# Half of the attention weights turned by VectorE blocks and a DMA round trip in every attention, with the transfers pinned to one order

## The chip, the cores and the metric

The kernel runs on one core of a Trainium2 chip. The metric is device time in microseconds for one execution; a lower number is better. The matrix engine is PE (TensorE), the others DVE (VectorE), ACT (ScalarE), POOL (GpSimd) and SP (SyncE, whose queue issues all the transfers here). Data are fp32 throughout.

## The reference, cut to what matters

A tensor x of 8 batches x 256 tokens x 512 features goes through four layers, conditioned on a vector per batch:

```python
# layer 0: rotary attention, 8 query heads of 64, one key/value head; then a gated MLP
h = ada_rms(x, time_emb, ln1_w, ln1_tw)
q, k, v = apply_rope(heads(h @ Wq.T)), apply_rope(heads(h @ Wk.T)), heads(h @ Wv.T)
x = x + (softmax(q @ k.T / sqrt(64)) @ v) @ Wo.T
x = x + (silu(h2 @ Wg.T) * (h2 @ Wu.T)) @ Wd.T
# layer 1: attention with 16 heads of 32 and a bias, gated by gamma; then an MLP with gelu
p = softmax(qn @ kn.T + attn_bias); x = x + ((p @ v) @ Wproj.T + bproj) * gamma1
# layer 2: 16 query heads of 32 in 4 groups of keys; a sparse mask (window, every 64th key, no later block of 128)
scores = where(mask, -inf, q @ k_exp.T / sqrt(32)); x = x + (softmax(scores) @ v_exp) @ Wo.T
# layer 3: eight experts on 64 features each, a conditioned layer norm, an output product
```

What matters here is the softmax in the three attentions: its weights come out with queries on the partitions and keys along the row, and the product with v needs them with keys on the partitions, so every 128 x 128 block of weights has to be turned.

## The kernel before, in words

x stays on chip as 16 tiles of 128 tokens x 512. A batch is two of them (TB = 2, S = 256, KC = 4 chunks of features). The layers run one after the other; each attention is one call of `attend` (L667 on), each MLP one call of `mlp`, whose products are Strassen-like (L1002, L1051) and keep PE full.

**One attention.** `attend` loops over B x n_groups steps; a group is four heads (two groups a batch in attention0, four in attention1 and attention2). Step i does, in program order: the scores of its group (`scored`, L692, four heads at once on row tiles of PE); the first half of the PE transposes of the group before (`turned`, L769 and a copy back by DVE or ACT, L478 or L481); the softmax of its group; a share of the other work (`some`); the second half of the transposes; another share; the weighted sum of the group before (`weighted`, L794) and its division (`divided`, L811); a third share. The other work is a queue of generators: the projection of the next batch (`project0/1/2`, products L628, transposes of queries and keys L1236, L1242, L1453), the output product of the batch before, loads. `some(us)` draws from it until its budget is used or until a generator yields None; `rest()` runs it to the end, whatever it yields, and is called when a batch begins.

**Softmax.** Per head and query tile: a maximum (DVE, L714, or with bias or mask by a fused DVE instruction, L730), then exponentials with a running sum (ACT, L734). In attention0 and attention1, except in the last batch, heads 0 and 1 of a group are written in an order of 32 x 32 blocks, with the keys of the scores permuted to match; DVE then turns all blocks at once (L739, one STREAM_TRANSPOSE of 128 x 1024), and two transfers complete the turn: four puts to a scratch tile in DRAM (`put`, L546, "flip<-p") and one fetch back (L743, "p<-flip"). Heads 2 and 3 are turned by PE. In attention2 all four heads are turned by PE: with its mask a head has three blocks of 128 x 128 (384 columns), not four. The reciprocal of the sums (L745) is turned by DVE (L749), put to DRAM (L752) and fetched broadcast (L757).

**Inputs of the projections.** The normalised input of a batch, turned to features on partitions, is hT. In attention1 and attention2 `prepare` makes it two batches ahead: statistics on DVE, a power on POOL, the scaled rows written in block order (L468), a DVE block transpose (L532), four puts (L546, "turn<-hT"), and `fetch` (L564, eight fetches "hT<-turn", or one where the next stage takes blocks). `modulate` scales and shifts it (L488 on DVE, L489 on ACT) at the end of a batch. One step of it is drawn per group.

**Rotary tables.** `angles` (L1164 to L1196) reduces positions times frequencies to within pi by a chain of DVE instructions (`less`, L1176) and takes sines on ACT. It runs for batch 0, for batch 1, and, from `conditions(0)`, for all other batches at once.

**Order.** A scheduler sets each engine's order before the run, from a simulation: an instruction traced later may be issued earlier when its inputs are ready sooner. `keep_in_program_order(i)` pins i behind the instruction traced just before it on the same engine, without a wait. Before, it pins the weighted sums of turned heads and the modulation, and no transfer. Buffers: four of "p" (128 x 1024 each), two of hT, three of "row", eight of "wbig", four PSUM banks each of A and C.

Of the kernel before, what the change touches and what calls it, by code (L numbers as in the profile page):

```python
# [42 lines left out]
    "n": 4, "hT": 2, "qT": 2, "kT": 2, "v": 2, "ctxT": 4, "p": 4, "qk": 4, "row": 3, "wbig": 8,  # L43
# [54 lines left out]
def constants():  # L98
# [15 lines left out]
        "mask2": np.ascontiguousarray(mask),  # L114
    }
# [63 lines left out]
class Program:  # L179
# [21 lines left out]

    def bank(self, tag):
        return self.t([P, 512], tag)
# [26 lines left out]
    def setup(self):  # L230
# [41 lines left out]
        self.flips = [self.tc.dram_tile([P, 8 * P], F32, name=f"flip{i}") for i in range(4)]  # L272
        self.n_flip = 0
        self.half_pi = c([P, 1], "half_pi")
# [156 lines left out]
    def normed(self, *args):  # L431
        steps = self.norms(*args)
        while True:
            try:
                next(steps)
            except StopIteration as e:
                return e.value

    def norms(self, xs, eps, rms=False, outs=None):

# [16 lines left out]
        nc.gpsimd.tensor_tensor(r, r, self.neg_half[:, 0:n], ALU.pow)  # L457
        rows = []
        for i, x in enumerate(xs):
            yield  # L460
# [4 lines left out]
            if rms:  # L465
                nc.vector.tensor_scalar(y, x, r[:, i : i + 1], None, ALU.mult)
            else:
                nc.vector.tensor_scalar(  # L468
                    y, x, mv[:, i, 0:1], r[:, i : i + 1], ALU.subtract, ALU.mult
                )  # L470
            rows.append(y)
        return rows

# [43 lines left out]
    def prepare(self, name, b, quick=False):  # L517

        eps, _, _, _, rms, blocks = self.stage(name)
        xs = [self.x[TB * b + t] for t in range(TB)]
        hT = self.t([P, KC * S], "hT")
        self.ready[name, b] = [hT, None, None, math.inf, False]
        if quick:
            self.ready[name, b][3] = 0
            self.ready[name, b][1] = self.normed(xs, eps, rms)
            return
        nc = self.nc
        y = hT.rearrange("p (c k t i) -> p c k t i", c=4, k=KC, t=TB)  # L530
        yield from self.norms(xs, eps, rms, [y[:, :, :, t, :] for t in range(TB)])
        nc.vector.transpose(hT, hT)  # L532
        kept = self.turns[self.n_turn % 3]
        self.n_turn += 1
        self.put(kept, hT)
        self.ready[name, b][2] = kept

    def in_blocks(self, name, b):

        return 2 if name != "attention2" and b < B - 1 else 0  # L540

    def put(self, kept, tile):

        to = kept.rearrange("(c i) (a x) -> a i c x", c=4, a=4)
        for a in range(4):
            self.nc.sync.dma_start(  # L546
                to[a], tile[32 * a : 32 * a + 32, :].rearrange("p (c x) -> p c x", c=4)
            )

    def fetch(self, calls):  # L550

        for (name, b), entry in self.ready.items():
            hT, _, kept, _, _ = entry
            if kept is None:
                continue
            entry[2:4] = None, self.calls + calls
            if self.stage(name)[5]:
                self.nc.sync.dma_start(hT, kept)
                continue
            parts = kept.rearrange("p (a k t j) -> p k t a j", a=4, k=KC, t=TB)  # L560
            to = hT.rearrange("p (k t a j) -> p k t a j", k=KC, t=TB, a=4)
            for k in range(KC):
                for t in range(TB):
                    self.nc.sync.dma_start(to[:, k, t], parts[:, k, t])  # L564
# [15 lines left out]
    def modulate(self):  # L580

        for (name, b), entry in self.ready.items():
            hT, rows, kept, at, done = entry
            if rows is None and not done and at < math.inf:
# [3 lines left out]
                entry[3:] = 0, True  # L588

    def h(self, name, b, quick=False):  # L590


        if (name, b) not in self.ready:
            for _ in self.prepare(name, b, quick):
                pass
            yield None
            self.fetch(1)
        hT, rows, _, at, done = self.ready[name, b]
# [53 lines left out]
    def attend(self, name, n_groups, hd, project, value, finish, work, key_tiles=(2, 2), biased=None,  # L652
# [25 lines left out]
        got, ctx = self.got, {}  # L678
# [19 lines left out]
        def softmax(s, b):  # L698
            n_blocks = self.in_blocks(name, b)
# [1163 lines left out]
```

## Time and profile before

| what | value |
|---|---|
| median of 3 runs | 2105.07 us (2104.76 to 2105.3) |
| the profiled execution | 2102.78 us |
| its span on the core, granted TensorE clock | 2100.7 us, 0.989 |
| attention0 with the start | 0 to about 306 us |
| MLP 0 | about 306 to 880 |
| attention1 | about 915 to 1270 |
| MLP 1 | about 1270 to 1655 |
| attention2 | about 1686 to 1941 |
| experts | about 1941 to 2101 |
| PE transposes of weights, L769 | 816, 122.3 us listed |
| DVE block transposes of weights, L739 | 42 |
| flips: puts, fetches | 168 and 42 |

The span runs from the first to the last instruction. Busy times of PE include overlapping matmuls once; the mean time of one matmul (282 ns at L769) is longer than the step from one to the next, since they are pipelined. The stage bounds are read from the chain of work that ended last. A "q" after an engine's name is its instruction queue: for SP, the issue of a transfer, not its landing.

### The profile page before, as it was taken

To read this page: it belongs to the slowest core of one execution; us is meant where nothing else is said; L and a number is where in the kernel's file an instruction comes from. 1 tells how busy PE (TensorE), PEld (TensorE's weight loads), DVE (VectorE), ACT (ScalarE), POOL (GpSimd) and SP (SyncE) were. 2 spreads that over 40 slices of the span, in tenths; PEclk is the share of its full clock that TensorE was granted. 3 is DMA by queue.
4 is the path that set the end of the run, shared out by engine and by line. 5 is a ranking of instruction groups with operands and counts; after the bars stand their busy time and mean duration, and the time that the engine had idled before them with its cause. 6 is when DMAs were issued, how large, how long until landed. Compare 5 with 4: busy or idle time off the path is not lost.

```text
span 2100.7 us, 36220 instructions
## 1 busy us (share of the span) xinstructions
PE 2034.6 (97%) x12946; PEld 1486.9 (71%) x12946; DVE 1348.9 (64%) x4432; ACT 743.7 (35%) x2330; POOL 302.7 (14%) x340
## 2 busy tenths in 40 slices
PE   7799999999999999999999999999999999999999
PEld 4455569999999999854544448999999755555444
DVE  6677766666676555756676675767666777676233
ACT  4233421111111111146566652222222265556543
POOL 1111200000000000054445621000000111010220
PEclk8999999999999999999999999999999999999999
DMA  9543451212130010335455542235211321210001
GB/s 317 161 139 94 115 202 39 72 42 64 62 108 26 16 32 16 97 95 140 130 145 142 150 132 87 86 92 155 63 46 36 89 44 38 58 38 21 9 36 40
DMA packets 202659, 182.48 MB, mean 87 GB/s; under 512 B 81200, under 2 KB 169200, under 8 KB 202480
## 3 DMA queue, kind: packets, MB, share of 16 engines
q1 hardware_dynamic: 202480, 180.17, 29.3%
q8 instruction: 103, 1.69, 0.3%
q14 instruction: 76, 0.62, 0.1%
HBM read 122.16 MB, written 57.97 MB: 86 GB/s over the span
## 4 chain that ended last, share of the span: by engine, by line
PE 82%; DVE 6%; ACT 6%; DMA 3%; POOL 2%; issue 1%; SPq 0%; ACTq 0%; DVEq 0%; POOLq 0%
PE C L1002 28%; PE C L628 21%; PE A L1051 18%; ACT p L734 4%; PE A L692 4%; PE C L794 3%; PE C L769 3%; PE A L1731 1%; PE C L1750 1%; ACT p L481 1%; DVE st L448 1%; DVE p L730 1%; DMA hT<-turn 1%; PE C L315 1%; DVE n L647 1%
## 5 line engine op out<-in xcount | busy, mean ns | idle before, releaser
L1002 PE MATMUL C<-hT,wbig 128*128 128x128 f32 x3072 | 416.4, 275 | 1.0 <-DVE p L1025 1.0
L1002 PEld LDWEIGHTS C<-hT,wbig 128*128 128x128 f32 x3072 | 388.7, 192 | 10.1 <-issue 3.5
L628 PE MATMUL C<-wqkv,hT 128*128 128x512 f32 (+1 forms) x768 | 314.7, 551 | 0.4 <-ACT v L1490 0.4
L734 ACT ACTIVATE p<-p,low 128x256 f32<-128x256 f32 (+1 forms) x512 | 240.0, 471 | 165.8 <-DVE low L730 154.5
L1051 PE MATMUL A<-wbig,p 128*128 128x256 f32 x1024 | 242.2, 379 | 0.0
L628 PEld LDWEIGHTS C<-wqkv,hT 128*128 128x128 f32 x768 | 131.7, 193 | 122.7 <-issue 108.7
L1051 PEld LDWEIGHTS A<-wbig,p 128*128 128x128 f32 x1024 | 189.7, 190 | 23.1
L1032 DVE TENSOR_TENSOR p<-p,C 128x256 f32<-128x256 f32 x192 | 79.0, 419 | 164.3 <-PE C L1002 162.3
L1022 ACT COPY p<-C 128x128 f32<-128x128 f32 x192 | 50.8, 265 | 367.5 <-PE C L1002 359.0
L628 PE MATMUL C<-wo,ctxT 128*128 128x512 f32 x336 | 159.8, 609 | 2.9 <-DVE ctxT L811 2.9
L1002 PE MATMUL C<-ctxT,wbig 128*128 128x128 f32 x1152 | 160.0, 275 | 0.0
L1002 PE MATMUL C<-qk,wbig 128*128 128x128 f32 x1152 | 159.8, 275 | 0.0
L456 POOL TENSOR_SCALAR r<-mv 128x2 f32<-128x2 f32 (+1 forms) x28 | 7.0, 252 | 967.7 <-DVE mv L449 967.7
L730 DVE CUSTOM_DVE_ANT_0 p<-A,row 128x256 f32<-128x256 f32 (+1 forms) x400 | 127.8, 377 | 26.6 <-PE A L692 24.9
L1002 PEld LDWEIGHTS C<-ctxT,wbig 128*128 128x128 f32 x1152 | 144.1, 192 | 0.0
L1002 PEld LDWEIGHTS C<-qk,wbig 128*128 128x128 f32 x1152 | 144.0, 192 | 0.0
L769 PEld LDWEIGHTS C<-ident,p 128*128 128x128 f32 x816 | 92.2, 142 | 64.3 <-issue 37.8
L769 PE MATMUL C<-ident,p 128*128 128x128 f32 x816 | 122.3, 282 | 4.8 <-DVE p L478 1.9
L1374 ACT ACTIVATE p<-C 128x128 f32<-128x128 f32 x64 | 17.7, 277 | 302.4 <-DVE p L1032 302.4
L1023 DVE TENSOR_TENSOR p<-p,C 128x128 f32<-128x128 f32 x192 | 54.7, 285 | 96.6 <-ACT p L1022 95.6
L628 PEld LDWEIGHTS C<-wo,ctxT 128*128 128x128 f32 x336 | 59.5, 191 | 67.7 <-issue 55.2
L734 ACT ACTIVATION_READ_ACCUMULATOR p<-p,low 128x1 f32 x512 | 96.2, 188 | 0.0
(227 smaller groups left out, 3224.6 us busy)
## 6 DMA issues: line engine op xcount, KB each, us to landing
flip<-p SPq DMA_DIRECT2D x168, 128.0 KB
p<-flip SPq DMA_DIRECT2D x42, 512.0 KB
turn<-hT SPq DMA_DIRECT2D x120, 128.0 KB
hT<-turn SPq DMA_DIRECT2D x16, 512.0 KB
kept<-hT SPq DMA_DIRECT2D x16, 512.0 KB
hT<-kept SPq DMA_DIRECT2D x16, 512.0 KB
wbig<-spread SPq DMA_DIRECT2D x64, 128.0 KB
hT<-turn SPq DMA_DIRECT2D x112, 64.0 KB
```

The source lines that it names most:

```text
L315: self.nc.tensor.matmul(m[32 * i : 32 * i + 32, :], cond[:, k, :], w[c // 512][:, k, c % 512 : c % 512 + width], start=(k == 0), stop=(k = ...
L628: self.nc.tensor.matmul(out, lhsT(k), rhs(k), start=(k == 0), stop=(k == n - 1))
L692: nc.tensor.matmul(s[j][:, at[q] : at[q] + wide[q]], lhsT(q), keys, start=True, stop=True,)
L730: nc.vector.tensor_tensor_reduce(out, src, by, -1.0, BIG, ALU.add, ALU.min, low[:, q : q + 1])
L734: nc.scalar.activation(out, src, AF.Exp, bias=low[:, q : q + 1], scale=sign, accum_out=tot[:, j, q : q + 1],)
L769: nc.tensor.transpose(m[:, n * P : (n + 1) * P], p[:, at[q] + k * P : at[q] + (k + 1) * P], self.ident,)
L794: mm = nc.tensor.matmul(o[i * hd : (i + 1) * hd, c * S + q0 * P : (c + 1) * S], value(got[b][1], g, j, k), weights(j, mine), start=(k == 0 ...
L1002: nc.tensor.matmul(m[:, c : c + P], w[:, k * P : (k + 1) * P], b[:, k], start=(first and k == 0), stop=(k == steps - 1), skip_group_check= ...
L1022: nc.scalar.copy(g[:, 0, :], m[:, 0:P])
L1023: nc.vector.tensor_tensor(g[:, 0, :], g[:, 0, :], m[:, P : 2 * P], ALU.add)
L1032: nc.vector.tensor_tensor(g[:, 1:3, :], g[:, 0, :].unsqueeze(1).to_broadcast([P, 2, P]), m[:, 2 * P : 4 * P].rearrange("p (i t) -> p i t", ...
L1051: nc.tensor.matmul(acc[at][:, half * S : (half + 1) * S], left, right, start=(p == 0 and half == 0), stop=(p == 3), skip_group_check=True,)
```

## The change

1. **Attention2 turns half of its weights by blocks too**: `in_blocks` now gives 2 in all attentions but in the last batch; a second copy of the mask in block order is a new constant (`mask2_blocks`) and is loaded once. The mask and the small rotary table now share one "row" tile. The DVE transpose there is 128 x 768, its put and fetch 384 KB each.
2. **Transfers are pinned** by `queued`: puts of weights and of hT, fetches of both, the put and the broadcast fetch of the reciprocals. In a softmax the order is: puts of the weights; the put of the reciprocals; one step of a preparation; the fetch of the weights; the broadcast fetches.
3. **`prepare` goes in five steps**: statistics; scaling and block transpose; puts; the first half of the fetches; the second half. The first two are drawn after a softmax, the others inside one. For batch b + 3 it begins at the last group of batch b; `fetch` is gone.
4. **"p" is one tile of eight parts** of 512 columns, given out in a ring (`part`); a softmax takes four parts, a step of an MLP two.
5. **`angles` has become a generator** (`angle_steps`) with three yields, and each `less` is pinned.

The core of the diff:

```diff
+    def part(self, n):
+        if self.n_part == 0:
+            self.parts = self.t([P, 8 * 512], "p")
+        at = self.n_part % 8
+        self.n_part += n
+        return self.parts[:, at * 512 : (at + n) * 512]
...
+    def queued(self, dma):
+        return self.tc.keep_in_program_order(dma)
...
-        return 2 if name != "attention2" and b < B - 1 else 0
+        return 2 if b < B - 1 else 0
...
     def prepare(self, name, b, quick=False):
...
+        by = self.norms_of(xs, eps, rms)
+        yield
+        hT = self.t([P, KC * S], "hT")
...
+        self.over(xs, by, rms, [y[:, :, :, t, :] for t in range(TB)])
         nc.vector.transpose(hT, hT)
+        yield
         kept = self.turns[self.n_turn % 3]
         self.n_turn += 1
         self.put(kept, hT)
+        yield
+        if blocks:
+            self.queued(nc.sync.dma_start(hT, kept))
+        else:
...
             for k in range(KC):
                 for t in range(TB):
+                    self.queued(nc.sync.dma_start(to[:, k, t], parts[:, k, t]))
+                if k == KC // 2 - 1:
+                    yield
+        entry[2] = self.calls + 1
...
                 if j == 3 and n_blocks:
                     nc.vector.transpose(blocks, blocks)
...
                     self.put(kept, blocks)
-                    nc.sync.dma_start(blocks, kept)
+                    between.append((blocks, kept))
...
-            nc.sync.dma_start(kept.rearrange("c (b r) -> b c r", b=4), inv_t)
+            self.queued(nc.sync.dma_start(kept.rearrange("c (b r) -> b c r", b=4), inv_t))
+            for steps in preps:
+                if len(steps) <= 3:
+                    next(steps.pop(), None)
+            preps[:] = [steps for steps in preps if steps]
+            for to in between:
+                self.queued(nc.sync.dma_start(*to))
...
+                for steps in preps:
+                    if len(steps) > 3:
+                        next(steps.pop())
+                if ahead_of and g == 0 and b == 0:
+                    for _ in self.prepare(name, 1, quick=True):
+                        pass
+                    preps.append([self.prepare(name, 2)] * 5)
+                    for _ in range(2):
+                        next(preps[-1].pop())
+                elif ahead_of and g == n_groups - 1 and b + 3 <= B:
+                    if b + 3 < B:
+                        preps.append([self.prepare(name, b + 3)] * 5)
+                        next(preps[-1].pop())
+                    elif after is not None:
+                        preps.append([self.prepare(after, 0)] * 4)
+                        next(preps[-1][-1])
+                elif not ahead_of and g == 0 and b == B - 1:
+                    preps.append([self.prepare(after, 0)] * 4)
+                    for _ in range(3):
+                        next(preps[-1].pop())
...
         def less(out, k, c):
-            nc.vector.scalar_tensor_tensor(out, k, -c, ang, ALU.mult, ALU.add)
+            self.tc.keep_in_program_order(
+                nc.vector.scalar_tensor_tensor(out, k, -c, ang, ALU.mult, ALU.add)
+            )
...
-                self.angles(self.cos, self.sin, slice(2 * TB, NT))
+                yield from self.angle_steps(self.cos, self.sin, slice(2 * TB, NT))
...
+        both = self.bank("row")
...
+        self.mask = both[:, TB * 64 :]
         nc.sync.dma_start(self.mask, d["mask2"])
+        self.mask_blocks = self.bank("row")[:, :384]
+        nc.sync.dma_start(self.mask_blocks, d["mask2_blocks"])
...
-            biased=(self.mask,), extra={7: (self.expert_inputs(0), 1.74)},
+            biased=(self.mask, self.mask_blocks), extra={7: (self.expert_inputs(0), 1.74)},
```

## The prediction

> **What bounds the kernel now.** I read the page's first part, then the table by stage, then the timeline of one batch of attention2, then the chain of waits in its last group.
>
> ```profile
> PE 2034.6 (97%) x12946; PEld 1486.9 (71%) x12946; DVE 1348.9 (64%) x4432; ACT 743.7 (35%) x2330; POOL 302.7 (14%) x340
> ```
>
> PE is busy in 97% of the span, so time goes down only where PE loses work or idles. The stages, from the table of busy time by stretch (columns: stretch, length, then busy us and count of PE, PEld, DVE, ACT and POOL, the granted clock, DMA share, GB/s):
>
> ```profile
> 0.00:80.00 80.00, 54.00 (x311) 31.16 (x312) 51.91 (x176) 26.66 (x65) 12.53 (x32) 0.85 0.70 239
> 915.00:1270.00 355.00, 348.11 (x1910) 173.40 (x1911) 241.95 (x810) 207.25 (x665) 166.04 (x144) 0.99 0.49 135
> 1686.00:1941.00 255.00, 241.44 (x1719) 132.97 (x1716) 182.59 (x834) 147.18 (x586) 26.54 (x34) 1.00 0.17 40
> ```
>
> Attention1 (second row) already turns half of its weights by blocks and leaves PE idle for 7 us in 355, with the DMAs at 135 GB/s. Attention2 (third row) turns all by PE, idles 13.6 us in 255 and moves 40 GB/s. So PE bounds both, and attention2 has room on the DMAs. Its batches repeat every 34.44 us (the chain shows the same piece at 1746.87, 1781.31, 1815.75). In one of them, PE's timeline:
>
> ```profile
> 1753.46 0.94 PE L692 MATMUL A<-kT,qT 32*128 32x128 f32 x16
> 1754.33 0.88 PE L769 MATMUL C<-ident,p 128*128 128x128 f32 x6
> 1755.04 1.88 PE L628 MATMUL C<-wo,ctxT 128*128 128x512 f32 x4
> ...
> 1756.76 0.88 PE L769 MATMUL C<-ident,p 128*128 128x128 f32 x6
> 1757.56 0.48 PE L692 MATMUL A<-kT,qT 32*128 32x128 f32 x2
> ...
> 1759.89 0.86 PE L794 MATMUL C<-p,kT 128*32 128x256 f32 x16
> ```
>
> A group is scores (L692), six transposes (L769), products, six transposes, the weighted sum (L794). Six transposes last until the next start 0.71 us later, 118 ns each, though a single one is listed with 280 ns: they overlap.
>
> **What goes.** The page has 816 transposes at L769. Attention2 has 8 batches x 4 groups x 4 heads x 3 blocks = 384; in batches 0 to 6 two heads of four leave: 7 x 4 x 2 x 3 = 168. Over five batches (1712.65 to 1884.62) I summed the time from each L769 start to PE's next start: 30.89 us for 240, 128.7 ns each, small waits included. 168 x 128.7 ns = **21.6 us**. It is between 168 x 110 ns = 18.5 (the bare step between two) and 21.6.
>
> The Trainium skill speaks against the swap: "VectorE: DVE Perf Modes", Rules for kernel authors, says to transpose 128x128 on TensorE when PSUM will do; The three transpose paths gives 390 ns there against 311 ns on VectorE, for 32x32 blocks alone. At its 390 ns the sum would be 65 us saved; the trace's step is a third of that, and it decides.
>
> **What comes, beside other work.** VectorE per batch of attention2: the copies of two heads a group go (eight, 4.4 us), four STREAM_TRANSPOSE of 768 columns come. The trace has 1024 columns at 1.245 us and 32 at 0.204, so 768 is about 0.98: 3.9 us. Net -0.5 us on an engine with 24.7 busy of 34.4: nothing. ScalarE keeps eight copies of 384 columns a batch, since the two heads left both go to it: nothing. Scores and weighted sums read in block order: in attention1, where heads 0 and 1 do so already, four row-tiled matmuls of 256 columns take 196 to 220 ns with blocks or without: nothing. DMA: 28 groups x 2 x 393 KB = 22 MB in some 240 us, 92 GB/s on top of 40, less than attention1 carries: nothing in bandwidth. The ring for p has the room of the four buffers before (four of eight parts a softmax, as two of four tiles): nothing. Mask and rotary table share a tile; the count of row buffers is the same: nothing.
>
> **The rotary steps.** PE's longest stall is 10.31 us at 57.26, because ScalarE's sine (L1193) stands ahead of two copies and waits 16.3 us for VectorE:
>
> ```profile
> 47.69 1.28 ACT L1193 ACT_TABLE_LOAD   x1
> 65.27 0.52 ACT L1193 ACTIVATE row<-row 128x384 f32<-128x384 f32 x1 [16.30 <-DVE row L1192]
> ```
>
> Each pinned `less` is tied to VectorE's instruction traced just before. By the code `conditions(0)` is drawn first inside `rest()` at batch 1, which doesn't stop at a yield, so that is the chain's own predecessor, which it needs anyway. The pins order nothing new. Bounds: -10.3 (the stall goes) to +10.3 (another such order in the neighbouring softmax). I take 0, because the chain and what is around it are traced as before.
>
> **What is late next: the last group.** The four groups' scores start at 1745.02, 1753.46, 1762.59, 1769.73, the next batch's at 1779.46. The chain of waits in the last one:
>
> ```profile
> 1771.08 1.86 ACT p L734 x8
> ...
> 1773.30 1.77 ACT p L734 x8
> 1775.08 0.02 issue
> 1775.10 0.04 DVE inv L745
> ...
> 1776.01 0.34 DVE n L647
> 1776.36 0.07 issue
> 1776.42 1.28 POOL qk L1650
> 1777.70 0.04 issue
> 1777.75 0.67 PE C L1236 x4
> ```
>
> Here PE isn't the limit: exponentials, VectorE's rope behind the reciprocal, POOL's sum, and only then the transposes of the next queries. Taking six transposes out of this iteration brings nothing: 7 x 6 x 128.7 ns = **5.4 us** of the 21.6 don't arrive. (Bounds: 0, were the scheduler to put rope first; 7 x 0.98 = 6.9 more, were the block transpose to stand in this chain.)
>
> **The blocks' way.** A way in attention1, on SP's queue:
>
> ```profile
> 1099.54 1.75 SPq L546 DMA_DIRECT2D flip<-p  x4
> 1101.40 0.55 SPq L752 DMA_DIRECT2D spread<-invT  x1
> ...
> 1103.31 0.34 SPq L743 DMA_DIRECT2D p<-flip  x1
> ```
>
> The scores were at 1093.66; the transpose ran 1098.27 to 1099.52; the last put was issued 1100.85 to 1101.30 and the fetch at 1103.31; the chain elsewhere shows a fetch landing in 3.38 us. For attention2, with T the start of a group's scores: two heads' maxima by T+2.1 and exponentials by T+3.3, transpose until T+4.5 (ScalarE's row: about 0.88 us a head), puts issued until T+6.3. The pinned order now is: puts, spread (T+6.3 to 6.9, since exponentials end at T+5.2 and the reciprocal's transpose at T+6.1), one step of a preparation, then the fetch. That step is four puts of hT (0.45 us each) or four fetches (0.61 each, the row of L564: 628 ns), so the fetch is issued at T+8.5 without one, T+8.7 after puts, T+9.3 after fetches, and lands some 2.9 us later, T+11.4 to T+12.2. Scores to own weighted sum lasts now 14.9, 15.5, 11.7 and 14.9 us; with 0.7 us less an iteration 13.4, 14.0, 10.3 and 13.5. Only the third group is short, by 1.9 us. PE already idles there for 0.54 + 0.73 us a batch, so I charge 1.9 - 1.27 = 0.6 x 7 = **4.4 us** (bounds 0, if PE's static order puts products first, and 1.9 x 7 = 13).
>
> "DMA: Bandwidth & Descriptors" of the Trainium skill, Anatomy of one DMA, gives 2.0 us and bytes at 436 GB/s for one DMA, so 2 x 2.9 = 5.8 us there and back. By that estimate the third group would land at T+10.3, just in time, and the 4.4 us would fall away; the trace's two trips, 2.5 and 3.4 us after issues that queue, are what I count.
>
> **hT.** Its fetch used to float (in attention2 issued at 1757 to 1764.6, long before the next batch's products at 1781.15). Pinned, its second half goes behind the spread of the last group. In attention1: 1135.05 + 4 x 0.61 = 1137.5; packets of such a fetch end 1.7 us after the last issue; 0.4 us for the modulation (L488): 1139.6. The products start at 1138.43 and need that half after two steps of 0.45 us, at 1139.3. Short by 0.3 to 0.8 us, five batches: I charge 0.4 x 5 = **2 us** (bounds 0 and 4). In attention2 it is ready at T+9.3+1.7+0.4 = T+11.4 and needed at T+9.0 (next scores) + 0.94 + 0.4 (three transposes) + 0.43 = T+10.8; the 0.6 us it lacks is covered by the delay charged above, uncovered it costs 0.6 x 5 = 3. Behind such a wait PE's queue holds the weighted sum, pinned after those products; on VectorE and ScalarE the modulation, pinned too, holds up the next softmax where it stands before it.
>
> Attention0 keeps its transposes and blocks; pinning puts its flips behind loads that preceded them before too (flip at 150.47, after the weights' loads): 0, bounds -3 and +10.
>
> **Sum.** -21.6 + 5.4 + 4.4 + 2 = -9.8 on the profiled execution's 2102.78 us (span 2100.7): 2093.0. The median of the runs shown, 2105.07, is 2.29 higher: **2095 us**.
>
> **Rivals.** *All of it arrives:* the scheduler fills every wait: 2105 - 21.6 = 2083; without the sine's stall too, 2073. For it: attention1 shows no PE gap over 0.15 us in its middle batches. Against it: attention2 has 16.4 us of products a batch to fill with, attention1 28.5. *It cancels out,* the change waits taking the transposes' place: the last group's chain takes the block transpose (6.9), the third group's charge doubles (8.8): 2105 - 21.6 + 5.4 + 6.9 + 8.8 + 2 = 2106, no change. *Slower: SP's one queue in a fixed order.* The fetch of each group stands behind the preparation's issues, which themselves wait for transposes and landings; where such a wait is 2 us longer than reckoned, the three groups of a batch that have one hold PE up by 2 us each: 6 x 6 = 36 us in attention2 against 16 gained, 2125. It decides from about 2.3 us a batch on, 0.8 us for each of the three. For it: puts of hT took 3.1 us to land (issued until 1753.96, fetch at 1757.15) and in attention1 fetches already held a flip back by 3 us (1112.68 to 1115.87). Against it: those cost PE nothing.
>
> **Chances.** Forecast 0.42 (2089 to 2100), all of it 0.22 (2070 to 2089), cancels 0.12, slower 0.24 (2110 to 2130). Two tenths per cent, 4.2 us, is about what a measurement here can tell from no change. So faster 0.64, same 0.12, slower 0.24. The range leaves out the tip of the gain and the upper half of the slower case: 2075 to 2118; the likeliest case's own is 2089 to 2100.
>
> **What would show it.** L769 at 648 instead of 816; in attention2 a period of 32.5 to 33.5 us; waits of L794 for p<-flip in third groups; the next queries' L1236 still behind POOL; the 10 us stall at 57 still there; small waits of L628 for hT in attention1. Wrong if the period stays at 34.4 or falls under 31.5, if the early stall vanishes, or if PE waits for flips in attention0 or 1.

## The result and the profile after

The changed kernel takes 2118.89 us (median of 4 runs, 2117.78 to 2123.94) against 2105.19 us before (4 runs beside it): a ratio of 1.0063, 95% interval 1.0039 to 1.0087. It is slower, by some 13 us, where 2095 was forecast. The profiled execution is the longest of the four, 2123.94 us, with a span of 2122.1 and a granted TensorE clock of 0.981 (before 0.989); so the trace shows some 5 us more loss than the median has.

Three rows first, from the page's busy times, its list of groups and its DMA issues, of the changed kernel:

```profile
PE 2027.6 (96%) x12778; PEld 1479.0 (70%) x12778; DVE 1351.5 (64%) x4404; ACT 746.6 (35%) x2330; POOL 304.8 (14%) x340
...
L790 PE MATMUL C<-ident,p 128*128 128x128 f32 x648 | 102.7, 286 | 7.0 <-DVE ctxT L833 3.6
...
p<-flip SPq DMA_DIRECT2D x28, 384.0 KB
```

The work did leave: 168 transposes fewer (L790 is L769 of before), 28 fetches of 384 KB more, PE busy for 7 us less. Yet the span grew by 21. So PE idles. The table of busy time by stretch, for the same three stages (columns as in the prediction; the stretches are moved and lengthened with the stages):

```profile
0.00:80.00 80.00, 54.60 (x300) 32.05 (x302) 50.76 (x173) 26.12 (x63) 12.58 (x32) 0.85 0.71 244
916.00:1280.00 364.00, 352.31 (x1931) 174.58 (x1931) 240.26 (x811) 207.90 (x665) 167.17 (x145) 0.99 0.52 136
1695.00:1962.00 267.00, 231.25 (x1551) 123.61 (x1550) 185.62 (x808) 148.65 (x585) 28.64 (x36) 0.94 0.50 124
```

Attention2 (third row) leaves PE idle for 36 us of 267, where it was 13.6 of 255, and the granted clock fell there from 1.00 to 0.94. A lower clock beside a less busy PE is the second thing to see in this row. For all that follows I take each attention from its first to its last scores: attention1 went from 336.8 to 343.5 us, attention2 from 263.2 to 275.1. Another 4 us are in attention0, which differs by as much between executions with the same order of instructions (below).

What PE waited for in attention2, from the waits of before and of after (us in total, times, longest):

```profile
PE C L1236 <- POOL qk L1650: 4.4, 6, 0.8
PE C L794 <- ACT p L481: 4.1, 7, 0.8
PE A L692 <- DVE low L730: 3.6, 1, 3.6
```

```profile
PE C L816 <- ACT p L491: 11.0, 7, 2.5
PE C L816 <- DMA p<-flip: 5.5, 2, 2.8
PE A L709 <- DVE qT L489: 4.6, 5, 3.4
PE C L816 <- DVE st L449: 4.4, 1, 4.4
PE C L1276 <- DVE ctxT L833: 4.2, 3, 1.9
```

The weighted sum (L816, L794 of before) waited for 4.1 us; now for 20.9. One of these waits, in PE's timeline of after, in a last group (the weights are the third group's):

```profile
1789.74 0.60 PE L1690 MATMUL C<-wqkv,n 128*128 128x256 f32 x2
1792.77 1.28 PE L816 MATMUL C<-p,kT 128*32 128x256 f32 x16 [2.44 <-ACT p L491]
1793.98 1.11 PE L1270 MATMUL C<-ident,qk 128*128 128x128 f32 x4
1794.88 0.42 PE L1276 MATMUL C<-ident,kr 128*128 128x128 f32 x1
1795.10 1.06 PE L1270 MATMUL C<-ident,qk 128*128 128x128 f32 x4
1797.45 0.31 PE L1276 MATMUL C<-ident,kr 128*128 128x128 f32 x1 [1.29 <-DVE ctxT L833]
```

SP's queue shows why the sum had to wait:

```profile
1784.12 1.82 SPq L576 DMA_DIRECT2D flip<-p  x4
1786.05 0.55 SPq L766 DMA_DIRECT2D spread<-invT  x1
1786.64 2.56 SPq L558 DMA_DIRECT2D hT<-turn  x4
1789.36 0.50 SPq L772 DMA_DIRECT2D p<-flip  x1
```

The four fetches of hT take 2.56 us to issue, ahead of the fetch of the weights. That one lands 3.22 us after its issue (the chain of waits), at 1792.58; the copy of the two heads that PE turned, put behind the exponentials on ScalarE, ends at 1792.77. The view puts the wait down to the copy, but the fetch alone would have held the sum as long: third groups wait in batches 0 to 5, 17.3 us in all, and in all six the sum begins 0.13 to 0.14 us after the last record of the fetch's landing in the trace. Behind the wait the weighted sum lasts 1.28 us instead of 0.86 and four L1270 1.11 instead of 0.66: PE runs at half clock (the records of the clock have 0.50 from 1793.14 to 1796.55).

### The profile page after: what moved, and what is told of

It is laid out like the page before. It is cut to its first block, busy times and chain, and to the rows that moved or that the text cites. A ratio compares the mean times of both kernels' runs of the same rounds, so it can differ in the third digit from the quotient of the medians.

```text
span 2122.1 us, 36171 instructions
## 1 busy us (share of the span) xinstructions
PE 2027.6 (96%) x12778; PEld 1479.0 (70%) x12778; DVE 1351.5 (64%) x4404; ACT 746.6 (35%) x2330; POOL 304.8 (14%) x340
## 3 DMA queue, kind: packets, MB, share of 16 engines
q1 hardware_dynamic: 222784, 202.40, 33.3%
## 4 chain that ended last, share of the span: by engine, by line
PE 81%; DVE 7%; ACT 4%; DMA 4%; POOL 2%; issue 1%; SPq 1%; ACTq 0%; DVEq 0%; POOLq 0%
PE C L1028 28%; PE C L645 21%; PE A L1077 18%; PE A L709 4%; ACT p L748 3%; PE C L816 3%; PE C L790 2%; PE A L1769 1%; DVE p L744 1%; PE C L1788 1%; DMA hT<-turn 1%; DMA p<-flip 1%; DMA wbig<-spread 1%; DVE st L449 1%; DVE hT L474 1%
## 5 line engine op out<-in xcount | busy, mean ns | idle before, releaser
L645 PE MATMUL C<-wqkv,hT 128*128 128x512 f32 (+1 forms) x768 | 319.2, 554 | 4.7 <-DVE hT L498 2.7
L645 PEld LDWEIGHTS C<-wqkv,hT 128*128 128x128 f32 x768 | 131.9, 194 | 127.8 <-issue 105.7
L645 PE MATMUL C<-wo,ctxT 128*128 128x512 f32 x336 | 159.0, 608 | 3.2 <-DVE ctxT L833 2.6
L790 PEld LDWEIGHTS C<-ident,p 128*128 128x128 f32 x648 | 75.0, 143 | 62.3 <-issue 39.9
L790 PE MATMUL C<-ident,p 128*128 128x128 f32 x648 | 102.7, 286 | 7.0 <-DVE ctxT L833 3.6
L645 PEld LDWEIGHTS C<-wo,ctxT 128*128 128x128 f32 x336 | 59.7, 191 | 67.7 <-issue 52.9
L709 PE MATMUL A<-kT,qT 32*128 32x256 f32 (+2 forms) x896 | 90.6, 406 | 8.5 <-DVE low L744 4.9
```

The source lines that it names most:

```text
L645: self.nc.tensor.matmul(out, lhsT(k), rhs(k), start=(k == 0), stop=(k == n - 1))
L709: nc.tensor.matmul(s[j][:, at[q] : at[q] + wide[q]], lhsT(q), keys, start=True, stop=True,)
L790: nc.tensor.transpose(m[:, n * P : (n + 1) * P], p[:, at[q] + k * P : at[q] + (k + 1) * P], self.ident,)
```

## Theories and experiments

Two theories stood at the beginning. **O**: the pinned order of transfers costs the time (the slower rival). **R**: the round trip of the weights is too long for attention2 in any order. A third came after the first four runs. **F**: it is too long for the third group only, and the half clock behind its wait adds to the price. Whether **the rotary pins** matter is answered by unpinned, which keeps them.

All were timed beside the kernel before (medians 2104.64 to 2106.41), except gaps, which measures a cost by itself. Attention1 and attention2 are from first to last scores in one profile, idle is PE's in attention2, "busy at half" is PE's busy time there under half clock.

| kernel | median us | ratio (95%) | attention1 | attention2 | idle | busy at half |
|---|---|---|---|---|---|---|
| before | 2105.19 | | 336.8 | 263.2 | 16.3 | 6.0 |
| after | 2118.89 | 1.0063 (1.0039 to 1.0087) | 343.5 | 275.1 | 38.6 | 34.3 |
| blocks_alone | 2108.11 | 1.0012 (1.0003 to 1.0021) | 336.1 | 266.0 | 31.6 | 25.1 |
| no_blocks2 | 2108.65 | 1.0016 (1.0008 to 1.0025) | 342.4 | 266.7 | 16.8 | 11.4 |
| unpinned | 2105.38 | 0.9993 (0.9983 to 1.0002) | 335.2 | 263.4 | 33.3 | 23.5 |
| flip_first_early | 2117.4 | 1.0057 (1.0044 to 1.0070) | 343.7 | 270.5 | 31.0 | 35.9 |
| skip3_unpinned | 2097.07 | 0.9962 (0.9949 to 0.9974) | 335.7 | 258.0 | 21.0 | 19.8 |
| skip3_pinned | 2113.47 | 1.0041 (1.0028 to 1.0054) | 342.4 | 269.2 | 28.9 | 24.1 |
| free_hT | 2122.79 | 1.0084 (1.0071 to 1.0098) | 341.4 | 275.9 | 38.0 | 38.2 |
| pin_hT | 2114.46 | 1.0047 (1.0035 to 1.0060) | 345.7 | 269.0 | 34.0 | 35.6 |
| pin_flips | 2102.90 | 0.9991 (0.9982 to 1.0000) | 334.2 | 263.0 | 33.1 | 26.1 |
| skip3_old | 2096.99 | 0.9964 (0.9951 to 0.9976) | 336.7 | 258.5 | 24.8 | 16.8 |
| skip23_unpinned | 2094.85 | 0.9948 (0.9936 to 0.9961) | 335.3 | 254.8 | 17.6 | 10.6 |

Where attention2's time stands, from first scores of a batch to first scores of a later one, in us:

| kernel | first batch | five middle batches | last two |
|---|---|---|---|
| before | 37.4 | 171.9 | 53.9 |
| after | 43.4 | 176.8 | 55.0 |
| blocks_alone | 40.9 | 162.9 | 62.2 |
| unpinned | 39.7 | 167.8 | 55.9 |
| skip3_unpinned | 37.9 | 163.5 | 56.5 |
| skip3_old | 38.2 | 164.7 | 55.6 |
| skip23_unpinned | 36.1 | 165.6 | 53.0 |

### One half of the change at a time: blocks_alone and no_blocks2

The kernel before, with blocks in attention2 and nothing else of the change but the mask in block order and the tile it shares:

```diff
-        return 2 if name != "attention2" and b < B - 1 else 0
+        return 2 if b < B - 1 else 0
```

> The kernel before with nothing but attention2's half in blocks (and its second mask); transfers unpinned, preparation in the old steps. Theory O (the order of the transfers costs the time: the flip's fetch behind a preparation's issues, hT's second half too late): attention1 stays at 43.6 us a batch, attention2 falls from 34.4 to about 33, total 2094 to 2100. Rival R (the round trip through DRAM is too long for attention2's short groups in whatever order): attention2 at 35 to 36 a batch with a wait of 2 us or more before the third group's weighted sum, total 2108 to 2116.

The changed kernel with that line put back, so that attention2 is turned by PE:

```diff
-        return 2 if b < B - 1 else 0
+        return 2 if name != "attention2" and b < B - 1 else 0
```

> The changed kernel with attention2 turned by PE as before; all the rest of the change stays. O and R alike: attention1 at 45.1 us a batch, some 8 us lost there by the end of it. O: attention2 at 34.5 to 35.5 (hT half a microsecond late), total 2112 to 2117, so blocks are worth nothing or less only in this order. R: attention2 at 34.4, total 2110 to 2113, and blocks cost 5 us or more here as they do in the old order.

Each alone costs some 2 us against the 2106.41 measured beside them; together they cost 13.7. They get in each other's way, so neither R nor O alone explains the result. That blocks_alone gains nothing though 168 transposes left it, in an order that pins no transfer, speaks for R or F. But its middle batches do gain, 9.0 us in five, where R had 35 to 36 us for a batch; what eats the gain is lost in the first batch (3.5) and the last two (8.3). PE's waits in its attention2:

```profile
PE C L795 <- DMA p<-flip: 12.9, 8, 5.0
```

For no_blocks2 both theories had forecast more, 2110 us at least. Where it loses is plain: its attention1 takes 342.4 us, as after's does, and its attention2 3.5 us more than before's; its span grew by 4.8 only, so some 4 us came back elsewhere, and where is open but for 2 us in attention0 (241.2 against 243.2).

### No pinned transfers: unpinned

```diff
     def queued(self, dma):
-        return self.tc.keep_in_program_order(dma)
+        return dma
```

> The changed kernel with no transfer pinned (traced order, steps of the preparation and blocks unchanged). O by the pins: fetches of hT float forward, attention1 back to 43.6 to 44 a batch, attention2 to 33 to 34.5, total 2097 to 2105. O by the steps (hT's second half is traced too late for the scheduler to bring it forward, pinned or not): attention1 stays near 45, total 2112 to 2118. R: attention2 above 35 either way.

No measurable difference from before, and 13 us faster than after: beside blocks in attention2, the pins of transfers cost all of the loss (without these blocks, in no_blocks2, they cost 2 us). Attention1's steady batches are back at 43.63 us (after 45.10). O holds for that. But attention2 still takes 263.4 us; the gain of the transposes is not there: its third groups still wait 14.9 us in all, against 17.3 in after. So the 11.7 us that the pins cost attention2 are not chiefly these waits. They lie in the first batch (3.7) and the middle ones (9.0). After's PE idles there 5.3 us more than unpinned's and works 10.8 us more at half clock; which waits bring that stays open.

### The weights' fetch ahead of hT's: flip_first_early

```diff
+            for to in between:
+                self.queued(nc.sync.dma_start(*to))
             for steps in preps:
                 ...
-            for to in between:
-                self.queued(nc.sync.dma_start(*to))
...
                 for t in range(TB):
                     self.queued(nc.sync.dma_start(to[:, k, t], parts[:, k, t]))
-                if k == KC // 2 - 1:
-                    yield
```

> The changed kernel, pins kept, with two moves: in a softmax the weights' fetch goes before the preparation's step, and both halves of hT are fetched in one step, at the third group. O: attention1 at 43.6 to 43.9 a batch (7 us back), attention2 at 33.5 to 34.5 (the third group's wait down from 2.4 to about 1.5 us), total 2100 to 2107. R: attention1 back, attention2 still above 35, total 2110 to 2113.

Neither theory had this (2100 to 2113): it only moves the loss. Attention1's steady batches are back at 43.62 us, but its first and last take longer and the stage 343.7. In attention2 the weights still come late (5.9 us), and now the scores wait for the queries, 12.3 us in all where after has 4.6:

```profile
PE A L707 <- DVE qT L489: 12.3, 6, 3.8
PE C L814 <- DMA p<-flip: 5.9, 3, 2.6
```

Eight fetches of hT take 5.3 us to issue, once a batch; whichever goes second is late.

### The third group left to PE: skip3_unpinned, skip3_pinned, skip3_old

In attention2's third group all four heads are turned by PE again (g is handed through); 126 transposes are gone instead of 168. First in unpinned, then in after, then in the kernel before (blocks_alone):

```diff
-    def in_blocks(self, name, b):
+    def in_blocks(self, name, b, g):
-        return 2 if b < B - 1 else 0
+        return 2 if b < B - 1 and (name != "attention2" or g != 2) else 0
```

> The changed kernel with no transfer pinned, and with attention2's third group of each batch turned by PE (126 of the 168 transposes still leave). Theory F (what is left of the loss is the third group's flip, whose scores come only 10 us before its weighted sum, and the half clock that follows PE's wait for it): waits for flips in attention2 from 15.6 us to under 5, half-clock time there from 27 to under 15 us, attention2 from 263 to 249 to 254 us between its first and last scores, total 2090 to 2097. Rival R (flips are too long for any of these groups): waits move to the other groups, attention2 at 260 or more, total 2101 to 2108.

> The changed kernel, pins kept, with attention2's third group turned by PE. F: the waits of about 2.5 us before the third group's weighted sum go, attention2 from 275 to 258 to 264, attention1 stays at 45.1 a batch; total 2103 to 2110. R: attention2 stays over 270, total 2114 or more.

> The order of before, with blocks in attention2 for all groups but the third; no other part of the change. Theory F (what made blocks worthless was the third group's late fetch and the half clock behind it): attention2 falls from 263.2 to some 258 us as it does when the same is done without pins in the changed kernel (258.0, ratio 0.996), so 2098 us, ratio 0.995 to 0.998. Rival S (the new five-step preparation, not the pins, is what makes the room): attention2 stays at 263 to 266 us as with blocks in all groups, ratio 1.000 to 1.002.

F holds in the main: with fewer blocks the unpinned kernel falls by 8 us, and blocks_alone by 11, so the new five-step preparation (rival S) has no part in it. In parts it does not. In skip3_unpinned PE still spends 23.9 us at half clock, where F had under 15. And from blocks_alone to skip3_old the five middle batches get slower by 1.8 us; the gain is in the first batch (2.7) and the last two (6.6). What is left of the waits for flips in skip3_unpinned:

```profile
PE C L1270 <- POOL qk L1688: 6.1, 6, 1.6
...
PE C L816 <- DMA p<-flip: 2.4, 3, 1.8
```

The steady batches of skip3_unpinned take 32.66 us, those of before 34.43: 1.77 us for 18 transposes, 98 ns each, nearly the bare step of 110. In skip3_pinned, slower than F's 2103 to 2110, there are still 9.9 us of waits of third groups' sums, with no transfer in their way: they wait for VectorE's copies of the heads that PE turned (at 1782.30 the copy stands behind the next group's maxima and block transpose). Attention1 keeps its 342.4. So with the pins the order on VectorE costs too, not only SP's queue; in skip3_unpinned the longest such wait is 1.2 us.

### Which pins: free_hT, pin_hT, pin_flips

Everything pinned but hT's fetches; only hT's fetches pinned; only the weights' puts and fetches and the reciprocals' transfers pinned (hT's puts and fetches float):

```diff
# free_hT
...
-                    self.queued(nc.sync.dma_start(to[:, k, t], parts[:, k, t]))
+                    nc.sync.dma_start(to[:, k, t], parts[:, k, t])
# pin_hT
...
+                    self.queued(nc.sync.dma_start(to[:, k, t], parts[:, k, t]), True)
...
-    def queued(self, dma):
-        return self.tc.keep_in_program_order(dma)
+    def queued(self, dma, pinned=False):
+        return self.tc.keep_in_program_order(dma) if pinned else dma
# pin_flips, as free_hT, and
-        self.put(kept, hT)
+        self.put(kept, hT, False)
...
+            if pinned:
+                self.queued(dma)
```

> The changed kernel with the fetches of hT (and of the MLP's input) unpinned, everything else pinned. If the pins' 14 us come from hT being fetched last: attention1 back to 43.6 a batch (8 us less), attention2 some us less since the flip's fetch no longer stands behind them, total 2104 to 2110. If they come from the order of flips and spreads: attention1 and attention2 as changed, total 2115 to 2119.

> The counterpart: the fetches of hT alone pinned, flips, puts and spreads free. If the cost is hT's: attention1 at 45 a batch, total 2112 to 2118. If it is the flips': attention1 at 43.6 to 44, total 2104 to 2108.

> The changed kernel with only the weights' puts and fetches and the reciprocals' transfers pinned; hT's puts and fetches float. In attention1 the batch took 43.63 us before, 45.10 after, 45.09 with hT's fetches alone pinned, 44.6 with everything but them pinned. Theory P (hT's puts hold up the fetches of weights and of hT behind them): without pinned puts of hT attention1 is back at 43.6 to 43.7 us a batch. Rival V (the pinned flips themselves keep hT's transfers out of their gaps): 44.4 to 44.7 as with the puts pinned. For attention2 both expect its loss to lie between unpinned (263.4) and all but the fetches pinned (275.9); the whole 2106 to 2120 us.

Attention1 answers clearly. Its steady batches took 43.63 us before, 45.10 after, 45.09 in pin_hT, 44.6 in free_hT and 43.63 in pin_flips. So hT's transfers cost when they are pinned, its puts or its fetches, and the weights' pins cost nothing. PE's waits between 950 and 1210 us, of after and of pin_flips:

```profile
PE C L645 <- DVE hT L498: 2.7, 4, 0.7
PE C L645 <- ACT hT L499: 1.7, 5, 0.6
```

```profile
PE C L816 <- ACT p L491: 0.7, 1, 0.7
PE C L645 <- ACT v L1525: 0.4, 1, 0.4
```

The waits for hT are gone. The fetches alone are not to blame, since free_hT is no faster than after (1.0084); why floating fetches behind pinned puts do no better in attention2 (275.9 us) than pinned ones (275.1) stays open.

pin_flips also shows that the third group is late without any pin of hT. Its SP queue and PE (scores of the group at 1760.74):

```profile
1764.95 1.75 SPq L575 DMA_DIRECT2D flip<-p  x4
1766.74 0.53 SPq L766 DMA_DIRECT2D spread<-invT  x1
1767.32 3.16 SPq L558 DMA_DIRECT2D hT<-turn  x4
1770.65 0.50 SPq L772 DMA_DIRECT2D p<-flip  x1
```

```profile
1770.54 0.60 PE L1690 MATMUL C<-wqkv,n 128*128 128x256 f32 x2
1773.94 1.27 PE L816 MATMUL C<-p,kT 128*32 128x256 f32 x16 [2.81 <-DMA p<-flip]
1775.14 1.12 PE L1270 MATMUL C<-ident,qk 128*128 128x128 f32 x4
```

Here too the scheduler issues hT's fetches in the gap between the weights' put and fetch; PE waits 2.81 us and then runs the sum in 1.27 us instead of 0.86. In attention2 the two meet in the queue, pinned or not: the third groups of pin_flips wait 15 us in all.

### Two groups only: skip23_unpinned

As skip3_unpinned, with blocks in the first two groups of attention2 alone (84 transposes gone):

```diff
-        return 2 if b < B - 1 and (name != "attention2" or g != 2) else 0
+        return 2 if b < B - 1 and (name != "attention2" or g < 2) else 0
```

> The changed kernel with its transfers unpinned, and blocks in attention2 for the first two groups only (the third and the last are turned by PE). Theory F and the accounting: 84 transposes of 112.5 ns leave, 9.5 us, against 126 and 14.2 us with three groups; idle time returns to before's 16 us from 21, half clock to 7 us from 24 (some 4.5 us less work lost). Net -9.5 + 0 + 0 to 2 against before, so attention2 254 to 256 us and 2094 to 2098 us. Rival L (the last group's blocks do no harm): attention2 at 261 to 263, 4.7 us of transposes back, and 2100 to 2103 us.

2094.85 us, against 2105.86 for before beside it: with 84 transposes fewer the gain is 11 us, where 168 gave none in unpinned (2105.38). It beats both kernels and has the lowest median of the study; its interval overlaps with that of skip3_unpinned (126 fewer, 2097.07). Idle time is nearly back to before's (17.6 against 16.3), and PE waits for little that it didn't wait for before:

```profile
PE C L1270 <- POOL qk L1688: 5.0, 6, 1.3
...
PE C L816 <- ACT p L491: 2.8, 6, 0.8
PE C L816 <- DMA p<-flip: 1.9, 3, 1.3
```

Its steady batches, 33.10 us, are longer than skip3_unpinned's by 0.44, as six transposes more should make them; it wins in the first batch (36.12 against 37.92) and the seventh (26.89 against 31.46), where skip3_unpinned has a wait of 2.6 us and then 6.8 us of half clock. So the last group's blocks do no harm in the middle of the stage; what they do at its ends is not separated. That two groups do better than three also says that "the third group only" was too narrow.

### The clock by itself: gaps

A kernel with blocks of 20 to 26 matmuls of 512 columns, each block behind a chain of VectorE steps that makes PE idle for a known time:

```python
for _ in range(20 + (3 * r + steps) % 7):
    nc.tensor.matmul(m, w[:, :P], self.x[1], start=True, stop=True)
...
nc.vector.tensor_tensor(got[:, :width], got[:, :width], self.x[2][:, :width], ALU.mult)
...
nc.vector.scalar_tensor_tensor(w[:, :width], got[:, :width], 0.0, self.x[0][:, :width], ALU.mult, ALU.add)
```

> This kernel leaves out all of the reference's computation but the copy of x to the output, and only measures PE's granted clock: 64 blocks of 20 to 26 fp32 matmuls of 512 columns, each block waiting for a chain of one to six VectorE steps on its predecessor's sum, so that PE idles for some 0.7 to 5 us between blocks of some 10 us. Theory W (a window): in the ten traces so far, on a fixed grid of 3.41 us, 38 of 38 stretches of attention2 in which PE was busy for under 0.4 were followed by half clock, and 12 of 745 in which it was busy for over 0.5. So gaps up to 1.7 us should never be followed by half clock, gaps from 1.9 us on in about (G - 0.4)/3.41 of the cases (0.59 at 2.4 us, 0.77 at 3.0), and gaps from 3.8 us on always. Rival I (an idle stretch): half clock only follows where a whole stretch is idle, so never below 3.41 us. Rival N (nothing to do with gaps): half clock comes as often behind short gaps as behind long ones.

| gap, us | 0.58 | 0.98 | 1.83 | 2.25 | 2.56 | 3.29 | 4.1 | 4.74 |
|---|---|---|---|---|---|---|---|---|
| number of gaps, of them followed by half clock | 8, 0 | 8, 0 | 8, 0 | 8, 5 | 8, 6 | 8, 7 | 8, 8 | 7, 7 |
| share that theory W expects | 0 | 0 | - | 0.54 | 0.63 | 0.85 | 1 | 1 |

W holds and both rivals fall. (The kernel ran once; the counts are from that one execution.) Two gaps of 2.25 us, one of each sort. PE's timeline, in two pieces, of gaps:

```profile
849.27 19.96 PE L1849 MATMUL C<-x,qk 128*128 128x512 f32 x42 [2.25 <-DVE qk L1859]
...
1034.76 20.84 PE L1849 MATMUL C<-x,qk 128*128 128x512 f32 x48 [2.25 <-DVE qk L1859]
```

And the first 3.41 us behind each, with the third stretch behind the first one, from its busy time by stretch (granted clock before the last two columns):

```profile
849.30:852.71 3.41, 3.41 (x5) 1.51 (x6) 0.00 (x0) 0.00 (x0) 0.55 0.00 0
...
856.12:859.53 3.41, 3.41 (x9) 1.52 (x8) 0.00 (x0) 0.00 (x0) 1.00 0.00 0
1034.80:1038.21 3.41, 3.41 (x8) 1.56 (x9) 0.00 (x0) 0.00 (x0) 1.00 0.00 0
```

The same gap, five matmuls in 3.41 us at a clock of 0.55 in the one case, eight in the other. On the grid on which the records of the clock begin and end, the first gap lies wholly in one stretch (846.24 to 849.65), in which PE was busy for 0.34; the second falls into two, with 0.57 and 0.77. PE counts as busy in both: the busy column doesn't show this loss, only the clock column and the durations do.

## Why the prediction was wrong, step by step

**What goes.** Right: L790 at 648. The slot was too large: 128.7 ns with small waits, where the steady batches of skip3_unpinned gave 98 ns and those of skip23_unpinned (34.43 - 33.10 = 1.33 us for 12) 111 ns. At the bare 110 ns, 168 are 18.5 us, the lower end of the bounds. (The 390 ns that the prediction set against this, from "VectorE: DVE Perf Modes" of the Trainium skill, The three transpose paths, are the page's figure for bf16; the data here are fp32.)

**The third group (4.4 us).** This is the step that failed first. The times were nearly right: from scores at 1779.91 the fetch was issued at T+9.45 and landed at T+12.7, forecast T+9.3 and T+12.2. But the 1.27 us by which PE already idled there was no cover: the whole lateness, 2.44 us, stands in the timeline. Of the 1.27 us, 0.73 were a wait behind the sum (for POOL); that one went, and waits of L1276 came in its place (6.0 us in the stage). Instead of 0.6 us a batch, 4.4 in all, the third groups of six batches wait 2.4 to 4.4 us each, 17.3 in all, beyond even the upper bound of 13. All waits of L816 rose from 4.1 to 20.9 us. And no step had a price for what follows: the reciprocal's division and L1276 late by 1.29 us more, and the clock.

**The clock.** Not in the prediction at all, and the second failure. In after's attention2 PE spends 41.0 us at half clock, twelve stretches of 3.41 us (before 6.8, two). PE is busy for 34.3 us of it, before 6.0. The weighted sum stretches from 0.86 to 1.28 us there; if all work does so, a third (1 - 0.86/1.28 = 0.33) of the added 28.3 us is lost, 9.3 us. That is an estimate; with it after's account of attention2 closes nearly: idle +22.3, clock +9.3, transposes -18.5, sum +13.1; measured +11.9. For blocks_alone the same sum gives 15.3 + 6.3 - 18.5 = +3.1 (measured +2.8), for skip3_unpinned 4.7 + 4.5 - 13.9 = -4.7 (-5.2). For pin_flips and unpinned it gives some 4 to 5 us too much (+4.9 and +4.2 against -0.2 and +0.2), so it is no better than that. F's "half clock" is then the smaller part: 9.3 us beside 22.3 of idle time.

**hT's late second half (2 us).** The mechanism was right, and pin_flips shows it: small waits of L645 for hT in attention1, which vanish when hT floats. The size was not: 1.47 us a batch instead of 0.4, 6.7 us for the stage (336.8 to 343.5), above its upper bound of 4. Only 4.4 us of it are waits for hT itself; the modulation that it needs on ScalarE stands, pinned, between exponentials (at 1102.82, behind five of them). In attention2 the "0.6 us it lacks" were held to be covered by the charge above; PE waited 1.9 us there for hT itself (before: not at all). The scores waited 4.6 us for late queries, but 3.4 of it is one wait at the last batch, which unpinned has too (3.8).

**The last group's iteration (5.4 us don't pay).** Not confirmed. In after PE's wait for POOL's sum there all but vanished, because PE came later itself; skip3_unpinned and skip23_unpinned give those transposes back to PE and have the waits for POOL again (6.1 and 5.0 us, before 4.4). No run took them out alone.

**Zeros.** DMA bandwidth: 124 GB/s in attention2, below attention1's 136; nothing here points to bytes. What counted is the time to issue on SP, the one queue of all transfers; the prediction had it nearly right for the third group (0.61 us a fetch of hT, measured 0.64 and more), but gave the order on the queue almost no price elsewhere. Rotary pins: 0 was right. unpinned keeps them and has the stall as before, 10.30 us. In after PE stands still at another place, for 7.45 us from 55.35 on (PE's timelines, unpinned first):

```profile
68.76 0.45 PE L1276 MATMUL C<-ident,kr 128*128 128x128 f32 x1 [10.30 <-ACT v L491]
```

```profile
62.81 3.50 PE L816 MATMUL C<-p,kT 128*64 128x256 f32 x16 [7.45 <-DVE row L1207]
```

The view names VectorE, but the sum begins 0.14 us after the last landing of its weights' fetch, as in attention2, and no_blocks2 and pin_flips have a wait of 7.4 us there that is put down to the fetch. So the pinned transfers make PE wait for flips in attention0, one of the signs that the prediction named; PE is busy for 54.60 of the first 80 us, 54.00 before, so in these 80 us nothing was lost by it. Attention0: 247.1 us against 243.2. But blocks_alone, which has before's order of instructions on every engine there, shows 247.3, and no_blocks2, which has after's, 241.2; no cause in the change is shown.

**The rivals.** The slower one, SP's one queue in fixed order, came true at 2118.9 (its price was 2125), but the nearness is in part luck, for it came with another count: not three groups a batch at 2 us each, but chiefly the third at 2.4, with half clock behind it, and hT's delay in attention1. Its argument against, that fetches had held flips back before without cost to PE, held for attention1 and was no evidence for attention2, where PE has less to fill with. "DMA: Bandwidth & Descriptors" of the Trainium skill, Anatomy of one DMA, would have had the weights back 5.8 us after their put, an estimate from its 2.0 us and bytes at 436 GB/s, which the page gives for transfers issued from GpSimd; these are issued from SP. In after, from the end of the puts at 1785.94, this is 1791.7; measured 1792.58, with the fetch standing until 1789.36 behind hT's. So the page's trip alone was not what failed.

Of what the prediction said would show, L790 at 648, the waits for flips in third groups and the waits for hT in attention1 came; the waits for POOL did not stay, the early stall changed its place, and the period of 32.5 to 33.5 us did not come: four batches took 35.5 to 36.3 us, over the 34.4 that it named as a sign that it is wrong.

## What to carry to other kernels

Where PE sets the time, price a wait of PE of about 2 us and more at the wait plus up to 1.7 us, half of a 3.41 us stretch (in gaps five matmuls ran in such a stretch, eight or nine in others), times its chance (5 of 8 at 2.25 us), and read the clock column beside the busy column: work taken from PE can come back as slower work. Take work away only where its replacement arrives in time: here blocks for two groups of four gained 11 us, for all four nothing. Before transfers are pinned into one order, add up their issue times on the queue between a put and its fetch, and look for what else must pass there; here the pins on the weights cost nothing, and those on the small transfers of hT, beside the blocks, cost 13 to 16 us (unpinned and pin_flips against after).

## What the runs showed of the hardware

**The clock is granted by stretches of 3.41 us on a fixed grid, by how busy PE was in the one before.** In attention2 of the ten traces that preceded gaps, 38 of 38 stretches at full clock in which PE was busy for under 0.4 were followed by a half one; of 745 with over 0.5, 12 were; between 0.4 and 0.5, 6 of 9. In each trace the records of the clock begin and end on one such grid. In gaps no idle time up to 1.84 us brought half clock (0 of 24), 18 of 24 between 2.25 and 3.29 did, and all 15 from 4.1 on. Laid on the grid of its clock records, gaps divides without exception: 34 stretches at full clock with PE busy for 0.41 or less were all followed by a half one, the 365 with 0.44 or more never.

"TensorE: Matmul & The Clock Gate" of the Trainium skill, Part 1, What's actually happening, gives a free-running window of 3413 ns, which these stretches agree with, and says that the half clock comes after at least one idle window. By that no gap below 3.41 us would matter. The runs show otherwise: a gap of 2.25 us, with PE working in the rest of the stretch, did it in 5 of 8 cases.

**Issue time on SP's queue depends on the transfer.** In after a row of four fetches of hT mostly lasts 2.56 us, 0.64 each, and up to 3.50; a put of weights mostly takes 0.44, a fetch of 384 KB 0.34 to 0.50 in the stretches read here.
